# Reading a row of 120 indices as three separated rows of 40 in the one-hot comparisons of a graph network

## The chip, the cores and the metric

The kernel runs on one core of one Trainium2 chip. The metric is device microseconds of one execution. A profile of one execution shows what each engine did: PE is TensorE (PEld its weight loads), DVE is VectorE, ACT is ScalarE, POOL is GpSimd, SP is SyncE. An instruction is named by its line in the kernel, and operands by the program's tile names.

## What is computed

The reference is a relational graph network of three layers with 6250 nodes, 256 features, 100000 edges sorted by their target node `dst`, 32 attributes per edge and 3 edge types, followed by a residual and a layer norm:

```python
ew = edge_attr @ edge_w + edge_b
rel_masks = [(edge_type == i) for i in range(3)]
inv_cnt = [1.0 / maximum(segment_sum(m, dst), 1.0) for m in rel_masks]
for l in range(3):
    msg = relu(x[src] * ew)
    out = 0
    for i in range(3):
        h = segment_sum(msg * rel_masks[i][:, None], dst) * inv_cnt[i][:, None]
        out = out + h @ weights[l, i]
    out = out + x @ roots[l] + biases[l]
    x = x + relu(out)
result = layernorm(x_in + x)
```

## The kernel before, in words

Edges are worked on 128 at a time; two such blocks make a pair, and two pairs (four blocks, 512 edges) make the group that most instructions handle at once. There are 391 pairs, so 195.5 groups in a layer and 586.5 in the three layers. All state but the node rows stays in SBUF.

For one pair, `gather_pair` (its DMA is line L1053) issues two indirect DMAs from POOL's queue, each of which fetches the 128 rows `x[src]` of one block; `xs` is the tile they land in, with eight buffers of one group each (for the first six pairs of a layer the rows are fetched early). For one group:

- `seed_ew` (L621, ScalarE) and `make_ew` (L634, TensorE) form the edge weights `ew_p` in PSUM;
- `weigh` multiplies them into the rows (L656, VectorE) and applies relu (L657, ScalarE); the last group of a layer is weighed in smaller pieces by `weigh_last` (L662, L663);
- `one_hot` (L669, VectorE) makes for each of the four blocks a matrix `oh` of 128 edges by `WK` = 120 columns. Column r*40+w is one where the edge has type r and its target is w nodes above the base of its span. It is one `tensor_scalar` per block: the row `iota_w` of the numbers 0 to 119, the same in every partition, is compared for equality with one number per partition, a column of `seg`. In layer 0 ScalarE also makes a bf16 copy `oh_b` (L673), from which the edges are counted;
- `reduce` multiplies rows and one-hot matrices on TensorE (L687 or L695) and so sums the messages by node and type into a PSUM tile `h_p`;
- for each span of nodes `add` (L723, VectorE) adds `h_p` into `acc`, a ring of nodes in SBUF.

Once a block of 128 nodes has all its edges, `node_mul` (L754) applies the weights, `node_end` (L785, L788) scales, adds and writes the new rows to `x_mid` in DRAM (L791), from which the next layer's gathers read. The root product goes through `root_turn`, `root_mul` and `root_keep` (L739). The last layer normalises (L794 to L806) and writes out.

The order on each engine is the order in which the Python code issues the instructions (`tc.manual_schedule()`): a loop over steps of one pair calls the functions above with fixed offsets. At step `it` the pair at position it+9 is gathered, it+3 weighed, it+2 one-hot encoded and it reduced. In a step VectorE gets the weighing first, then what belongs to nodes, then the one-hots of a group, and last the adds.

`iota_w` is made once, ahead of everything else, by one GpSimd iota instruction (L1081).

Of the kernel before, what the change touches and what calls it, by code (L numbers as in the profile page):

```python
# [8 lines left out]
F32 = mybir.dt.float32  # L9
# [433 lines left out]
def ordered_path(ctx, tc, x, attr_laid, A, weights, roots, biases, edge_w, edge_b, out, src, src_i, seg, place_i, consts, x_root,  # L443
# [6 lines left out]
    nc = tc.nc  # L450
    P = 128
    N, D = x.shape
    E = src.shape[0]
    L, R = weights.shape[:2]
# [5 lines left out]
    DC = D // P  # L460
    WK = R * WIN
    AHEAD = 9
# [3 lines left out]
    for u, (lo, hi) in enumerate(zip(least, most)):  # L466
        if u < order[0]:
            reach.append((ASIDE + lo, ASIDE + hi))
        elif lo // RING == hi // RING:
            reach.append((lo % RING, hi % RING))  # L470
        else:
            reach.append((0, RING - 1))
    ident, ones, iota_w = consts
# [33 lines left out]

    acc = big.tile([P, DC + 1, R, ASIDE + 2 * P + WIN], F32, name="acc")
    inv = big.tile([P, NT, R], F32, name="inv")
# [6 lines left out]
    for c in range(DC + 1):  # L516
        if c < DC // 2:
            nc.vector.memset(acc[:, c], 0.0)
        else:
            nc.scalar.activation(acc[:, c].rearrange("p r n -> p (r n)"),  # L520
                                 zero.to_broadcast([P, R * (ASIDE + 2 * P + WIN)]), AF.Copy)
    nc.vector.memset(x_all[:, NT - 1, :], 0.0)
# [27 lines left out]
    def closes(u):  # L550
        p = order.index(u)
        return p == U - 1 or span_of[order[p + 1]] != span_of[u]
# [34 lines left out]
    def layer(l, r_sb, b_sb, ats, early, pools):  # L587
# [11 lines left out]
        xs, ew_ps, ohs, h_ps, h_ss, o_ps, rs = {}, {}, {}, {}, {}, {}, {}  # L599
# [13 lines left out]
        def pairs_of(q):  # L613
            return range(min(2, U - 2 * q))
# [50 lines left out]
        def one_hot(q):  # L665
            ohs[q] = edge.tile([P, 4, WK], F32, name="oh", bufs=3)
            n = 2 * len(pairs_of(q))
            for t in reversed(range(n)):
                nc.vector.tensor_scalar(ohs[q][:, t, :], iota_w, seg[:, 4 * q + t:4 * q + t + 1], None,  # L669
                                        op0=ALU.is_equal)  # L670
            if l == 0:
                oh_bs[q] = edge.tile([P, 4, WK], BF, name="oh_b", bufs=3)
                nc.scalar.activation(oh_bs[q][:, :n], ohs[q][:, :n], AF.Copy)  # L673

        def reduce(u):
# [8 lines left out]
            if turned(span):  # L684
                for i in range(2):
                    t = u % 2 * 2 + i
                    nc.tensor.matmul(h_p[:WK, :D], ohs[u // 2][:, t, :], xs[u // 2][:, u % 2, i, :],  # L687
                                     start=(i == 0 and first), stop=(i == 1 and closes(u)), skip_group_check=True)
                    if l == 0:
                        nc.tensor.matmul(h_p[:WK, D:D + 1], oh_bs[u // 2][:, t, :], full_ones[:, 0:1],  # L690
                                         start=False, stop=(i == 1 and closes(u)), skip_group_check=True)
                return
            for i in range(2):
                for d in range(CH):
                    nc.tensor.matmul(h_p[:, d * WK:(d + 1) * WK],  # L695
                                     xs[u // 2][:, u % 2, i, d * P:(d + 1) * P] if d < DC else full_ones,
# [15 lines left out]
        def add(span):  # L712
            u = span[0]
            if places[:1] != [u // 8]:
# [6 lines left out]
                                       skip_runtime_bounds_check_because="it is a place in acc")  # L721
            there = acc[:, :CH, :, bass.ds(place, WIN)]
            nc.vector.tensor_tensor(there, h_ps[span][:, :CH * WK].rearrange("p (c r w) -> p c r w", c=CH, r=R), there, op=ALU.add)  # L723
# [36 lines left out]
        def slot_of(c):  # L760
            return c % (RING // P) * P if c > 1 else ASIDE + c * P

# [4 lines left out]
        def wrap():  # L767
            nc.vector.tensor_add(acc[:, :CH, :, :WIN], acc[:, :CH, :, :WIN], acc[:, :CH, :, RING:ASIDE])

        def clear(slot):  # L770
            nc.scalar.activation(acc[:, :CH, :, slot:slot + P],  # L771
                                 zero[:, :, None, None].to_broadcast([P, CH, R, P]), AF.Copy)
            if slot == 0:
                nc.scalar.activation(acc[:, :CH, :, RING:ASIDE], zero[:, :, None, None].to_broadcast([P, CH, R, WIN]),
                                     AF.Copy)
# [52 lines left out]
        for it in range(-11, max(starts) + 8):  # L828
# [75 lines left out]
            if pair(2) is not None and first_of(it + 2, 2) and pair(2) // 2 != order[-1] // 2:  # L904
                one_hot(pair(2) // 2)
            if pair(3) is not None and first_of(it + 3, 2) and pair(3) // 2 == order[-1] // 2:
                one_hot(pair(3) // 2)
# [12 lines left out]


WIN = 40
RING = 1024
ASIDE = RING + WIN
ROOTS = 24
# [81 lines left out]
def schedule(N, E, share):  # L1007

    P = 128
    U = -(-E // (2 * P))  # L1010
    NT = -(-N // P)
    K = first_pairs(N, E)
    spans = spans_of(N, E)
    order = order_of(N, E)
    added = {s: p + 1 for s, p in stages(N, E, share)[2].items()}
    done = []
    for c in range(NT):
        edges = E * min(1.0, (P * (c + 1) / N) ** 0.5)
        u = U if c == NT - 1 else min(U, -(-int(edges) // (2 * P)) + 4)
        done.append(max(added[s] for s in spans if s[0] >= K and (s[0] < u or s[0] == K)))  # L1020
    node = lambda e: int(N * min(1.0, max(0.0, e / E)) ** 2)
    least = [node(2 * P * u - ASTRAY) for u in range(U)]
    most = [node(2 * P * u + ASTRAY) for u in range(U)]
    moved = done[1] + 1
    starts = [0] * NT
    step = moved
    for c in range(2, NT):
        step = starts[c] = max(done[c] + 2, step + 4)
    starts[1] = max([step + 4] + [added[s] for s in spans if s[0] < K and any(most[u] + WIN > P for u in range(*s))])
    starts[0] = max(max(added.values()), starts[1] + 4)  # L1030

    for u, v in spans:
        p = added[u, v]
        if u >= K:
            assert all(p <= starts[c] or least[u] >= P * (c + 1) for c in range(2, NT))
            assert p <= moved or least[u] >= 2 * P
            assert all(p < starts[c] or least[u] >= P * c for c in range(8, NT, 8))
            for b in range(RING // P + 1, (most[u] + WIN - 1) // P + 1):
                assert (moved + 2 if b - RING // P == 1 else starts[b - RING // P] + 4) < p
        else:  # L1040
            assert most[u] <= 2 * P and (p <= starts[1] or most[u] + WIN <= P)
    return order, starts, moved, least, most
# [16 lines left out]
def kernel(ctx, tc, x, src, dst, edge_attr, edge_type, weights, roots, biases, edge_w,  # L1059
# [3 lines left out]
    nc = tc.nc  # L1063
    P = 128
# [4 lines left out]
    T = (E + P - 1) // P  # L1069
    T -= T % -2  # L1070
    U = T // 2
    WK = 3 * WIN
    K = schedule(N, E, 1)[0][0]

    keep = ctx.enter_context(tc.tile_pool(name="keep", bufs=1))
# [1 line left out]
    make_identity(nc, ident)  # L1077
    ones = keep.tile([1, P], F32, name="ones_o")
    nc.vector.memset(ones, 1.0)
    iota_w = keep.tile([P, WK], F32, name="iota_w")  # L1080
    nc.gpsimd.iota(iota_w, pattern=[[1, WK]], base=0, channel_multiplier=0,  # L1081
                   allow_small_or_imprecise_dtypes=True)
    node_i = keep.tile([P, 1], F32, name="node_i")
    nc.gpsimd.iota(node_i, pattern=[[0, 1]], base=0, channel_multiplier=1, allow_small_or_imprecise_dtypes=True)
# [1 line left out]
    seg = keep.tile([P, TC], F32, name="seg_o")  # L1086
# [6 lines left out]
    with tc.tile_pool(name="look", bufs=1) as look, tc.tile_pool(name="look_p", bufs=2, space=PSUM) as look_p, \  # L1093
# [27 lines left out]
        base = look.tile([1, U], F32, name="base")  # L1121
# [103 lines left out]
```

## Time and profile before

| | |
|---|---|
| median of 3 runs | 2968.16 us (2967.99 to 2969.02) |
| the profiled execution's own time | 2969.27 us |
| its span, first to last instruction | 2967.0 us |
| mean granted TensorE clock | 0.971 |
| what DMA moved | 387.39 MB, mean 131 GB/s |
| costliest VectorE line | L656, 711.5 us in 585 instructions |
| costliest ScalarE line | L657, 615.7 us in 585 instructions |

The profile counts an engine as busy only while one of its instructions runs. A group of instructions is shown with its number, its busy time in us, the mean duration of one in ns, and the idle time of the engine just ahead of them with what ended it; "issue" there is time in which the engine waited for nothing that the profile shows. In a timeline the first number of a row is the start in us from the start of the span and the second the time in us; rows of the same kind that follow each other are merged (x4), and the idle time before stands in brackets. The time of an execution is a little longer than the span, since it has work ahead of the first and behind the last instruction.

### The profile page before, as it was taken

To read this page: it belongs to the slowest core of one execution; us is meant where nothing else is said; L and a number is where in the kernel's file an instruction comes from. 1 tells how busy PE (TensorE), PEld (TensorE's weight loads), DVE (VectorE), ACT (ScalarE), POOL (GpSimd) and SP (SyncE) were. 2 spreads that over 40 slices of the span, in tenths; PEclk is the share of its full clock that TensorE was granted. 3 is DMA by queue.
4 is the path that set the end of the run, shared out by engine and by line. 5 is a ranking of instruction groups with operands and counts; after the bars stand their busy time and mean duration, and the time that the engine had idled before them with its cause. 6 is when DMAs were issued, how large, how long until landed. Compare 5 with 4: busy or idle time off the path is not lost.

```text
span 2967.0 us, 43407 instructions
## 1 busy us (share of the span) xinstructions
PE 2588.4 (87%) x13712; PEld 1780.6 (60%) x13712; DVE 1886.0 (64%) x4910; ACT 1502.6 (51%) x1911; POOL 2235.0 (75%) x2355
## 2 busy tenths in 40 slices
PE   5999999999998788888988998778888988999886
PEld 2666677777765545555666666454555666666644
DVE  6656577777774545556666666445556677778754
ACT  4666656556565444454444444434444444444443
POOL 7777777777777777777777777777777777777776
PEclk9999999999999999999999999989999999999999
DMA  5444444444444444444444444444444444444443
GB/s 168 147 145 136 147 123 124 128 130 130 127 135 128 132 116 120 128 121 123 127 125 130 130 131 128 135 132 124 126 133 133 135 132 132 139 136 137 128 127 96
DMA packets 173705, 387.39 MB, mean 131 GB/s; under 512 B 43594, under 2 KB 79068, under 8 KB 173468
## 3 DMA queue, kind: packets, MB, share of 16 engines
q0 software_dynamic: 112608, 307.65, 36.1%
q1 hardware_dynamic: 53280, 68.50, 7.2%
q10 hardware_dynamic: 7580, 8.37, 0.9%
q8 instruction: 113, 1.85, 0.3%
q14 instruction: 124, 1.02, 0.1%
HBM read 364.89 MB, written 19.46 MB: 130 GB/s over the span
## 4 chain that ended last, share of the span: by engine, by line
PE 43%; DMA 17%; POOL 15%; issue 13%; DVE 7%; ACT 4%; DVEq 0%; POOLq 0%; ACTq 0%
POOL xs L1053 15%; DMA xs<-x_mid,src_r 14%; PE h_p L695 11%; PE ew_p L634 10%; PE h_p L687 9%; PE o_p L754 7%; DVE xs L656 5%; DMA xs<-in_x_dram,src_io 3%; PE r_p L736 3%; ACT xs L657 2%; ACT ew_p L621 2%; PE r_p L728 1%; PE h_p L707 1%; DVE x_root L739 1%; DVE acc L723 1%
## 5 line engine op out<-in xcount | busy, mean ns | idle before, releaser
L1053 POOL DMA_INDIRECT xs<-x_mid,src_r x1540 | 1465.5, 952 | 469.2 <-issue 367.8
L657 ACT ACTIVATE xs<-xs 128x1024 f32<-128x1024 f32 (+1 forms) x585 | 615.7, 1052 | 1315.7 <-DVE xs L656 1301.3
L656 DVE TENSOR_TENSOR xs<-ew_p,xs 128x1024 f32<-128x1024 f32 (+1 forms) x585 | 711.5, 1216 | 772.8 <-DMA xs<-x_mid,src_r 490.1
L1053 POOL DMA_INDIRECT xs<-in_x_dram,src_io x770 | 733.3, 952 | 235.1 <-issue 192.8
L695 PEld LDWEIGHTS h_p<-oh,xs 128*128 128x128 f32 x5160 | 663.5, 194 | 242.9 <-issue 114.5
L695 PE MATMUL h_p<-oh,xs 128*128 128x120 f32 x5160 | 725.7, 285 | 82.2 <-issue 36.6
L634 PE MATMUL ew_p<-ew_sb,at 64*128 64x512 f32 x2346 | 686.2, 661 | 101.0 <-ACT ew_p L621 96.9
L687 PE MATMUL h_p<-xs,oh 128*120 128x256 f32 x2088 | 575.4, 410 | 19.5 <-issue 5.7
L621 ACT ACTIVATE ew_p<-seed 128x1024 f32<-128x1024 f32 x582 | 588.8, 1012 | 0.0
L669 DVE TENSOR_SCALAR oh<-iota_w,seg_o 128x120 f32<-128x120 f32 x2346 | 512.6, 296 | 0.0
L754 PE MATMUL o_p<-w_sb,acc 128*128 128x256 f32 (+1 forms) x1728 | 440.1, 391 | 34.6 <-DVE x_root L785 31.2
L687 PEld LDWEIGHTS h_p<-xs,oh 128*120 128x120 f32 x2088 | 367.2, 193 | 161.9 <-issue 51.3
L723 DVE TENSOR_TENSOR acc<-h_p,acc 128x240 f32 (+1 forms) x732 | 323.7, 442 | 191.0 <-PE o_p L754 70.5
L754 PEld LDWEIGHTS o_p<-w_sb,acc 128*128 128x128 f32 (+1 forms) x1728 | 308.1, 190 | 158.6 <-DVE x_root L785 71.4
L634 PEld LDWEIGHTS ew_p<-ew_sb,at 64*128 64x128 f32 x2346 | 181.3, 189 | 230.6 <-ACT ew_p L621 124.5
L785 DVE SCALAR_TENSOR_TENSOR x_root<-o_p,inv,x_root 128x256 f32<-128x256 f32 (+1 forms) x432 | 207.0, 479 | 27.9 <-PE o_p L754 21.0
L736 PE MATMUL r_p<-r_sb,t_s 128*128 128x256 f32 x588 | 161.6, 398 | 33.0 <-ACT t_s L732 32.2
L771 ACT ACTIVATE acc<-zero_o 128x768 f32<-128x768 f32 (+1 forms) x150 | 140.2, 934 | 14.6 <-PE o_p L754 13.9
L673 ACT ACTIVATE oh_b<-oh 128x480 bf16<-128x480 f32 x196 | 116.2, 593 | 45.3 <-DVE oh L669 43.6
L736 PEld LDWEIGHTS r_p<-r_sb,t_s 128*128 128x128 f32 x588 | 103.5, 193 | 54.8 <-ACT t_s L732 43.1
L728 PEld LDWEIGHTS r_p<-ident_o,x_all 128*128 128x128 f32 x294 | 30.7, 143 | 167.3 <-DVE x_root L739 121.0
L728 PE MATMUL r_p<-ident_o,x_all 128*128 128x128 f32 x294 | 65.0, 303 | 69.2 <-DVE x_root L739 68.9
(110 smaller groups left out, 942.8 us busy)
## 6 DMA issues: line engine op xcount, KB each, us to landing
at<-in_attr_laid_dram SPq DMA_DIRECT2D x147, 256.0 KB
xs<-x_mid,src_r POOLq DMA_INDIRECT x1540, 2.8
xs<-in_x_dram,src_io POOLq DMA_INDIRECT x770, 2.8
x_mid<-x_all SPq DMA_DIRECT2D x96, 128.0 KB
x_all<-in_x_dram ACTq DMA_DIRECT2D x8, 768.0 KB
x<-in_x_dram SPq DMA_DIRECT2D x48, 128.0 KB
out_dram<-x_all SPq DMA_DIRECT2D x48, 128.0 KB
w_sb<-in_L_gnn_weights_dram SPq DMA_DIRECT2D x3, 768.0 KB
```

Source lines behind the costliest of these rows:

```text
L621: nc.scalar.activation(ew_ps[q][:, :n], seed[:, None, :, :].to_broadcast([P, n, 2, D]), AF.Copy)
L634: nc.tensor.matmul(ew_ps[q][:, k].rearrange("p i d -> p (i d)"), at[half, :], ew_sb[half].rearrange("p i d -> p (i d)"), start=False, stop ...
L656: nc.vector.tensor_mul(there, ew_ps[q][:, pairs.start:pairs.stop], there)
L657: nc.scalar.activation(there, there, AF.Relu)
L669: nc.vector.tensor_scalar(ohs[q][:, t, :], iota_w, seg[:, 4 * q + t:4 * q + t + 1], None, op0=ALU.is_equal)
L687: nc.tensor.matmul(h_p[:WK, :D], ohs[u // 2][:, t, :], xs[u // 2][:, u % 2, i, :], start=(i == 0 and first), stop=(i == 1 and closes(u)), ...
L695: nc.tensor.matmul(h_p[:, d * WK:(d + 1) * WK], xs[u // 2][:, u % 2, i, d * P:(d + 1) * P] if d < DC else full_ones, (ohs if d < DC else o ...
L723: nc.vector.tensor_tensor(there, h_ps[span][:, :CH * WK].rearrange("p (c r w) -> p c r w", c=CH, r=R), there, op=ALU.add)
L736: nc.tensor.matmul(rs[c][:, 1, :], t_ss[c][:, d, :], r_sb[:, d, :], start=(d == 0), stop=(d == DC - 1))
L754: nc.tensor.matmul(o_p[:n, j, :], acc[:, d, r, slot:slot + n], w_sb[:, r * DC + d, :], start=(d == 0), stop=(d == DC - 1))
L785: nc.vector.scalar_tensor_tensor(root, o_p[:n, j, :], inv[:n, c, r:r + 1], root, op0=ALU.mult, op1=ALU.add)
L1053: nc.gpsimd.indirect_dma_start(out=xs[:, u % 2, i, :], out_offset=None, in_=x_rows[:, :], in_offset=bass.IndirectOffsetOnAxis(ap=src_i[:, ...
```

## The change

The tile `iota_w` gets three rows of 44 numbers in place of one row of 120. In each row the first 40 places hold the numbers (0 to 39, 40 to 79, 80 to 119), and the last 4 are never read or written. The comparison reads the three rows of 40, and its output is written as before, 120 numbers next to each other, now addressed as three rows of 40 that touch. The same numbers are compared with the same numbers.

```diff
@@ one_hot
             for t in reversed(range(n)):
-                nc.vector.tensor_scalar(ohs[q][:, t, :], iota_w, seg[:, 4 * q + t:4 * q + t + 1], None,
+                nc.vector.tensor_scalar(ohs[q][:, t, :].rearrange("p (r w) -> p r w", r=R), iota_w[:, :, :WIN], seg[:, 4 * q + t:4 * q + t + 1], None,
                                         op0=ALU.is_equal)
@@
 WIN = 40
+APART = WIN + 4
@@ tile_gnn_resnorm_kernel
-    WK = 3 * WIN
@@
-    iota_w = keep.tile([P, WK], F32, name="iota_w")
-    nc.gpsimd.iota(iota_w, pattern=[[1, WK]], base=0, channel_multiplier=0,
+    iota_w = keep.tile([P, 3, APART], F32, name="iota_w")
+    nc.gpsimd.iota(iota_w[:, :, :WIN], pattern=[[WIN, 3], [1, WIN]], base=0, channel_multiplier=0,
                    allow_small_or_imprecise_dtypes=True)
```

## The prediction

> **What bounds the kernel now.** I read the page's top and its chain of waits first.
>
> ```profile
> span 2967.0 us, 43407 instructions
> PE 2588.4 (87%) x13712; PEld 1780.6 (60%) x13712; DVE 1886.0 (64%) x4910; ACT 1502.6 (51%) x1911; POOL 2235.0 (75%) x2355
> PE 43%; DMA 17%; POOL 15%; issue 13%; DVE 7%; ACT 4%; DVEq 0%; POOLq 0%; ACTq 0%
> ```
>
> By busy share and by the chain, TensorE looks like the bound. The groups of line L1053, the gathers that POOL issues, say otherwise (busy us, mean ns, then idle us ahead; in the second view min/median/max ns, first and last start):
>
> ```profile
> L1053 POOL DMA_INDIRECT xs<-x_mid,src_r x1540 | 1465.5, 952 | 469.2 <-issue 367.8 <-ACT ew_p L621 35.7 <-PE r_p L728 11.0
> L1053 POOL DMA_INDIRECT xs<-in_x_dram,src_io x770 | 733.3, 952 | 235.1 <-issue 192.8 <-ACT ew_p L621 12.5 <-DMA xs<-in_x_dram,src_io 6.1
> L1053 POOL DMA_INDIRECT xs<-x_mid,src_r x1540: 942/947/1477, 1002.5 to 2951.0; - x193
> L1053 POOL DMA_INDIRECT xs<-in_x_dram,src_io x770: 942/946/1958, 19.1 to 986.3; - x193
> L1053 POOL DMA_INDIRECT x_root<-in_x_dram,src_f x12: 942/946/1111, 3.8 to 17.8; - x12
> L1053 POOLq EVENT_SEMAPHORE  x589: 17/43/6376, 16.8 to 2940.1; - x197
> ```
>
> The idle time is 469.2/1540 = 0.305 us for each gather of one group and 235.1/770 = 0.305 in the other: a fixed pause after each gather, not a wait. From the first start (3.8) to the last (2951.0), 2346 gathers follow each other at 2947.2/2345 = 1.257 us, against 0.947 + 0.305 = 1.252 for the median one. So POOL hands out gathers without a break from start to end, and all else follows: the "75%" is 952 of 1257 ns. The span is 3.8 us, the gathers, and 16.0 us of tail after the last one starts. Only what changes a gather's length, starves POOL, or lengthens the tail can move the time.
>
> What lengthens a gather? Its median is 947, its mean 952: 1465.5 - 1540 x 0.947 = 7.1 us and 733.3 - 770 x 0.946 = 4.9 us, together **12.0 us** above the median pace. I looked for these gathers in the timeline, and for Vector instructions that are stretched too:
>
> ```profile
> L669 DVE TENSOR_SCALAR oh<-iota_w,seg_o x2346: 249/275/520, 40.5 to 2952.6; 128x120 f32<-128x120 f32 x196
> L806 DVE TENSOR_SCALAR x_all<-x_all,mv x49: 411/413/648, 2118.6 to 2961.0; 128x256 f32<-128x256 f32 x48, 106x256 f32<-106x256 f32 x1
> L739 DVE TENSOR_TENSOR x_root<-r_p,b_sb x147: 404/414/416, 65.7 to 2737.6; 128x256 f32<-128x256 f32 x147
> L785 DVE SCALAR_TENSOR_TENSOR x_root<-o_p,inv,x_root x432: 466/482/486, 138.3 to 2958.8; 128x256 f32<-128x256 f32 x141, 106x256 f32<-106x256 f32 x3
> L788 DVE SCALAR_TENSOR_TENSOR x_all<-x_root,x_all x147: 424/425/499, 145.6 to 2959.3; 128x256 f32<-128x256 f32 x144, 106x256 f32<-106x256 f32 x3
> ```
>
> The two TENSOR_SCALAR lines, one SBUF input and an SBUF output, have a long upper tail (520 and 648 over medians of 275 and 413). L739 and L785, with one tensor in PSUM, have none (416 and 486). L788, with two in SBUF, has a short one. L669 is the one-hot comparison, and it is the line that the change rewrites. Both sides of the blocking are visible:
>
> ```profile
> 1438.30 1.07 DVE L669 TENSOR_SCALAR oh<-iota_w,seg_o 128x120 f32<-128x120 f32 x4
> 1438.38 0.95 POOL L1053 DMA_INDIRECT xs<-x_mid,src_r  x1 [0.30 <-PE ew_p L634]
> 1851.72 0.85 DVE L669 TENSOR_SCALAR oh<-iota_w,seg_o 128x120 f32<-128x120 f32 x4
> 1852.06 1.32 POOL L1053 DMA_INDIRECT xs<-x_mid,src_r  x1 [0.30 <-issue]
> ```
>
> In the first pair four one-hots take 1.07 us in place of 0.85 and the gather is untouched. In the second the one-hots keep 0.85 and the gather takes 1.32 in place of 0.95. Over the whole timeline, 231 gathers are over 8 ns longer than the median; 199 of them overlap a one-hot and carry 12.7 us of the 13.9 us of excess; in 169 of these (8.2 us) no other Vector instruction with two SBUF inputs or of the L806 kind overlaps, in 30 (4.6 us) one does.
>
> [...]
>
> **The change part by part.** (a) The index row gets gaps. POOL's one iota still makes 120 numbers:
>
> ```profile
> L1081 POOL IOTA iota_w<- 128x120 f32 x1 | 0.2, 226 | 0.0
> L1053 POOL DMA_INDIRECT x_root<-in_x_dram,src_f x12 | 11.6, 969 | 4.8 <-issue 3.4 <-DMA src_f<-in_src_laid_dram 1.5
> ```
>
> It stands ahead of the first gather, which waits 1.5 us for its indices: cost nothing; without that cover at most its own 0.2 us.
>
> (b) All 2346 one-hots read three rows of 40 that do not touch, and write 120 numbers that do. No trace row shows such a pair. [...]
>
> ```profile
> L577 DVE TENSOR_SCALAR src_r<-src_io 128x782 int32<-128x782 int32 x1 | 0.6, 558 | 0.0
> L578 DVE SCALAR_TENSOR_TENSOR src_r<-src_io,src_r 128x782 int32<-128x782 int32 x1 | 1.0, 974 | 0.0
> L669 DVE TENSOR_SCALAR oh<-iota_w,seg_o 128x120 f32<-128x120 f32 x2346 | 512.6, 296 | 0.0
> ```
>
> (974 - 558)/782 = 0.53 ns an element, x 120 = 64 ns: a one-hot goes from 275 to about 339 ns, four from 0.85 to 0.85 + 4 x 0.064 = 1.11 us. Today's mean for four is 512.6/586.5 = 0.874 with the blocking in it, so VectorE works 0.235 us more per four, 586.5 x 0.235 = 138 us, and reaches about 2024 us or 68%. The lower bound for (b) is nothing (rate unchanged). VectorE is not the bound, so in a steady stretch this hides under the 5.02 us that four gathers take.
>
> (c) Gathers are no longer blocked by one-hots. Bounds: nothing, and all 12.0 us. I take the 8.2 us, and half of the 4.6 (the two-input instructions stay): **-10.5 us**.
>
> (d) Where the longer one-hots show. POOL starves once, for a row tile at the start:
>
> ```profile
> 57.89 0.95 POOL L1053 DMA_INDIRECT xs<-in_x_dram,src_io  x1 [0.30 <-issue]
> 59.62 0.95 POOL L1053 DMA_INDIRECT xs<-in_x_dram,src_io  x1 [0.79 <-ACT t_s L732]
> ```
>
> That is 0.79 - 0.30 = 0.49 us, behind a chain with some four groups of one-hots since 40.5 us: 0 to 4 x 0.26 = 1.0 us more, taken **+0.5**. At the end of a layer the last rows of x_mid leave well before they are gathered:
>
> ```profile
> 996.44 0.33 SPq L791 DMA_DIRECT2D x_mid<-x_all  x1
> 1002.54 0.99 POOL L1053 DMA_INDIRECT xs<-x_mid,src_r  x1 [0.30 <-issue]
> DMA to landing us min/median/max: 2.6/2.8/6.8
> ```
>
> 6.1 us, less a landing (nearest row: the gathers' median of 2.8), cover one group's 0.26. In the tail the group stands between two weighings:
>
> ```profile
> 2951.01 0.95 POOL L1053 DMA_INDIRECT xs<-x_mid,src_r  x1 [0.30 <-issue]
> 2952.06 0.85 DVE L669 TENSOR_SCALAR oh<-iota_w,seg_o 128x120 f32<-128x120 f32 x4
> 2952.82 0.42 DVE L662 TENSOR_TENSOR xs<-ew_p,xs 128x256 f32<-128x256 f32 x1
> 2953.74 0.42 DVE L662 TENSOR_TENSOR xs<-ew_p,xs 128x256 f32<-128x256 f32 x1 [0.51 <-DMA xs<-x_mid,src_r]
> ```
>
> The second L662 waits 0.51 us for the last gather's landing, more than 0.26: nothing.
>
> Sum: -10.5 + 0.5 = -10.0 us. The profiled execution took 2969.27, 2.3 outside its span, and should become 2959.3; the median of the runs, 2968.16, is 1.1 lower, so **2958.2**.
>
> **Rivals.** [...]
>
> *B, layer 0 falls behind (slower).* TensorE is nearly full there, and the add into acc (L723), on which it waits, is queued on VectorE right behind the one-hots:
>
> ```profile
> 300.00:650.00 350.00, 333.91 (x2061) 243.93 (x2060) 246.04 (x624) 210.01 (x271) 264.99 (x280) 1.00 0.45 131
> 650.00:870.00 220.00, 211.73 (x1315) 155.67 (x1315) 164.30 (x418) 131.93 (x160) 166.68 (x176) 1.00 0.44 130
> PEld h_p L695 <- DVE acc L723: 22.4, 24, 1.9
> 817.33 0.22 PE L695 MATMUL h_p<-oh_b,full_ones 128*128 128x120 bf16 x1
> 826.84 0.96 POOL L1053 DMA_INDIRECT xs<-in_x_dram,src_io  x1 [0.30 <-ACT ew_p L621]
> ```
>
> PE is 95% and 96% busy; the third row is of 556 to 865 us. The last two are the tightest place after the start: the gather at 826.84 refills the tile that the matmul at 817.33 was last to read (found by counting the matmuls of L687 and L695), a margin of 9.3 us. From 300 to 870 us 113 groups pass; with the full 0.235 us on the path they lose 26.6 us, POOL stalls for 26.6 - 9.3 = 17.3, and the time is 2958.2 + 17.3 = 2975. Stalling begins above 0.08 us per group, a net loss above (9.3 + 10.0)/113 = 0.17. Against it: these are 24 waits in the 309/5.02 = 61 groups of their stretch; if the 0.235 reaches the path in those alone, it is 0.09 us per group, about where stalling begins and far from a loss.
>
> *C, part of the blocking stays*, because any Vector traffic from SBUF disturbs POOL: a third of the gain, 2965. L739 and L785 without a tail speak against it.
>
> **How the numbers follow.** Forecast 0.69, its own range 2955.5 (all 12.0 us and the 0.49) to 2963 (half the gain); A 0.13, B 0.10, C 0.08. The range 2955.5 to 2968.5 takes in the forecast, C and half of A. A change of 0.2% is 5.9 us, about what a measurement can tell: under 2962.2 lies nearly all of the forecast, 0.68; between that and 2974.1 lie A, C and a little of B, 0.22; above, 0.10.
>
> **What would show it.** Right: L669 at about 339 ns with hardly any spread between median and maximum; L1053's mean near 947 to 948 with the pause still 0.305; VectorE near 68%; the last gather starting near 2941. [...] Wrong by B: idle time ahead of L1053 above 0.305 a gather, between 600 and 900 us. Wrong by C: L669 at a narrow 339 and L1053's mean still 950 or more.

## The result, and the profile after

The changed kernel takes 2960.94 us in the median (2959.04 to 2962.46, 10 runs) against 2968.89 (2967.99 to 2970.57, 10 runs): a ratio of **0.9973, 95% interval 0.9965 to 0.998**, or 8.0 us less. The forecast was 10.0 us less. The profiled execution after, 2962.46 us, is the slowest of its ten runs and 6.8 us below the profiled one before, 2969.27. The rows below come from these two executions.

The profiled execution has a span of 2960.2 us in place of 2967.0. Its engines (the head of the page), and the gathers, whose line is now L1054: first their groups with busy us, mean ns and idle us, then min/median/max ns with first and last start.

```profile
span 2960.2 us, 43407 instructions
PE 2591.9 (88%) x13712; PEld 1782.6 (60%) x13712; DVE 1998.2 (68%) x4910; ACT 1503.8 (51%) x1911; POOL 2228.8 (75%) x2355
```

```profile
L1054 POOL DMA_INDIRECT xs<-x_mid,src_r x1540 | 1460.5, 948 | 469.1 <-issue 363.4 <-ACT ew_p L621 31.1 <-PE h_p L687 11.3
L1054 POOL DMA_INDIRECT xs<-in_x_dram,src_io x770 | 732.0, 951 | 234.6 <-issue 192.3 <-ACT ew_p L621 11.0 <-DMA xs<-in_x_dram,src_io 5.8
```

```profile
L1054 POOL DMA_INDIRECT xs<-x_mid,src_r x1540: 942/946/1455, 1000.9 to 2944.3; - x193
L1054 POOL DMA_INDIRECT xs<-in_x_dram,src_io x770: 942/946/2007, 19.1 to 984.5; - x193
```

Two things stand in these rows. VectorE works 1998.2 - 1886.0 = 112 us *more*, and the kernel is faster. And POOL's gathers are busy 1465.5 - 1460.5 = 5.0 and 733.3 - 732.0 = 1.3 us less, 6.3 together, with the pause after each still 469.1/1540 = 0.305 us. The last gather starts at 2944.3 in place of 2951.0, which is 6.7 of the span's 6.8 us: 6.3 are the shorter gathers, and the rest is the one starvation of POOL, 0.49 us at 59.62, which did not come back. The timeline of POOL after shows only the usual pause there.

```profile
58.45 0.94 POOL L1054 DMA_INDIRECT xs<-in_x_dram,src_io  x1 [0.30 <-issue]
59.69 0.95 POOL L1054 DMA_INDIRECT xs<-in_x_dram,src_io  x1 [0.30 <-issue]
60.95 0.95 POOL L1054 DMA_INDIRECT xs<-in_x_dram,src_io  x1 [0.30 <-issue]
```

The run with two rows apart, below, whose comparisons last as long as before, does not have that starvation either (0.30 us ahead of its gather at 59.45). So its absence is not shown to be the change's doing.

The durations of the rewritten comparison and of the three Vector lines beside it, in the form of the prediction's rows:

```profile
L669 DVE TENSOR_SCALAR oh<-iota_w,seg_o x2346: 303/327/335, 40.8 to 2946.2; 128x120 f32<-128x120 f32 x196
L806 DVE TENSOR_SCALAR x_all<-x_all,mv x49: 411/414/647, 2113.6 to 2954.3; 128x256 f32<-128x256 f32 x48, 106x256 f32<-106x256 f32 x1
L739 DVE TENSOR_TENSOR x_root<-r_p,b_sb x147: 406/414/417, 64.1 to 2731.6; 128x256 f32<-128x256 f32 x147
L788 DVE SCALAR_TENSOR_TENSOR x_all<-x_root,x_all x147: 424/425/483, 144.0 to 2952.6; 128x256 f32<-128x256 f32 x144, 106x256 f32<-106x256 f32 x3
```

L669 went from 249/275/520 to 303/327/335: longer in the median, and its tail is gone. L806, which was not touched, keeps its tail of 647.

**What a held gather looks like.** From the timeline after, two gathers that are still held, each with the Vector instruction that runs as it starts (start us, duration us):

```profile
98.41 1.35 DVE L765 TENSOR_TENSOR acc<-acc 128x1152 f32<-128x1152 f32 x1
98.57 2.01 POOL L1054 DMA_INDIRECT xs<-in_x_dram,src_io  x1 [0.30 <-PE h_p L690]
871.62 0.43 DVE L788 SCALAR_TENSOR_TENSOR x_all<-x_root,x_all 128x256 f32<-128x256 f32 x1
871.67 1.19 POOL L1054 DMA_INDIRECT xs<-in_x_dram,src_io  x1 [0.30 <-issue]
```

L788 ends at 872.05, 0.38 us into the gather, and the gather is 1.19 - 0.95 = 0.24 us too long. L765 ends at 99.76, 1.19 us into its gather, which is 1.06 us too long. Both fit one reading of these profiles: the gather's wait ends with the Vector instruction that is in progress some **0.13 us after the gather's start**. Being in progress there is not enough, however. In the profiles before, after and of the changed kernel once more (below), 166 gathers have an L788 alone in progress at that point. The 48 whose L788 had started 45 ns or more ahead of them are all longer, each by the L788's end less 0.13 us to within 12 ns. The 118 whose L788 had started later, from 42 ns ahead on, are at most 3 ns longer. (The limit is L788's own: after, two L768's that started 26 and 28 ns ahead did hold their gathers.) The seven L788's of the profiles before and after that are in progress at that point and started 2 to 42 ns ahead of the gather are themselves the longer ones (458 to 499 ns over a median of 425), here 0.48 in place of 0.43 us:

```profile
1898.15 0.48 DVE L788 SCALAR_TENSOR_TENSOR x_all<-x_root,x_all 128x256 f32<-128x256 f32 x1
1898.18 0.95 POOL L1054 DMA_INDIRECT xs<-x_mid,src_r  x1 [0.30 <-issue]
```

I sorted all gathers more than 8 ns over 947 by the Vector line in progress at that point. Before: 8.0 us of excess lie under L669 (164 gathers, alone or overlapping its neighbour), 1.7 under L788, 1.5 under L765, 0.4 under L768, 0.3 under L806. After: less than 0.1 under L669 alone, 2.7 under L788, 1.7 under L765, 0.9 under L768, 0.7 under L806. Of the gathers with an L669 alone in progress there, 131 of 338 were held before and 6 of 423 after, these by at most 12 ns.

### The profile page after: what moved, and what is told of

It is laid out like the page before. It is cut to its first block, busy times and chain, and to the rows that moved or that the text cites. A ratio compares the mean times of both kernels' runs of the same rounds, so it can differ in the third digit from the quotient of the medians.

```text
span 2960.2 us, 43407 instructions
## 1 busy us (share of the span) xinstructions
PE 2591.9 (88%) x13712; PEld 1782.6 (60%) x13712; DVE 1998.2 (68%) x4910; ACT 1503.8 (51%) x1911; POOL 2228.8 (75%) x2355
## 5 line engine op out<-in xcount | busy, mean ns | idle before, releaser
L1054 POOL DMA_INDIRECT xs<-x_mid,src_r x1540 | 1460.5, 948 | 469.1 <-issue 363.4
L1054 POOL DMA_INDIRECT xs<-in_x_dram,src_io x770 | 732.0, 951 | 234.6 <-issue 192.3
L695 PE MATMUL h_p<-oh,xs 128*128 128x120 f32 x5160 | 734.3, 287 | 86.4 <-issue 34.5
L669 DVE TENSOR_SCALAR oh<-iota_w,seg_o 128x120 f32<-128x120 f32 x2346 | 622.9, 327 | 0.0
```

The costliest lines, as they stand in the source:

```text
L669: nc.vector.tensor_scalar(ohs[q][:, t, :].rearrange("p (r w) -> p r w", r=R), iota_w[:, :, :WIN], seg[:, 4 * q + t:4 * q + t + 1], None, o ...
L695: nc.tensor.matmul(h_p[:, d * WK:(d + 1) * WK], xs[u // 2][:, u % 2, i, d * P:(d + 1) * P] if d < DC else full_ones, (ohs if d < DC else o ...
L1054: nc.gpsimd.indirect_dma_start(out=xs[:, u % 2, i, :], out_offset=None, in_=x_rows[:, :], in_offset=bass.IndirectOffsetOnAxis(ap=src_i[:, ...
```

## The experiments

All runs are compared with the kernel before on the same chip at the same time. A gather's ordinary length is not the same in all profiles: its median is 946 or 947 ns in the two above, in the second one of the changed kernel and in that of the kernel before with more comparisons, and 949 ns in the other five, of which one (two rows apart) has comparisons as long as before. Summed over the ordinary gathers (those not more than 8 ns over 947) that is some 4 to 6 us; so ratios are compared, not microseconds across sessions. The row of the run with the sum in PSUM, below:

```profile
L1055 POOL DMA_INDIRECT xs<-x_mid,src_r x1540: 942/949/1456, 1000.3 to 2945.6; - x193
```

**The changed kernel again**

> The changed kernel once more, as the mark for the others. Every theory: about 2961 us, ratio 0.997 to before; comparisons (L669) near 327 ns without a tail; gathers' mean near 949 ns.

Ratio 0.9973 (0.9963 to 0.9984), median 2967.02 us against 2974.61. L669 again without a tail:

```profile
L669 DVE TENSOR_SCALAR oh<-iota_w,seg_o x2346: 304/328/335, 39.5 to 2944.0; 128x120 f32<-128x120 f32 x196
L1054 POOL DMA_INDIRECT xs<-x_mid,src_r x1540 | 1459.5, 948 | 469.1 <-issue 362.2 <-ACT ew_p L621 32.6 <-DMA xs<-x_mid,src_r 11.0
```

The excess over 947 ns, summed over all gathers (those below it counted as negative), is 3.5 us here, 5.4 in the first profile of the same kernel, and 11.5 before. What is left depends on where in a gather the few remaining instructions fall.

**Two rows apart in place of three**

```diff
-  ohs[q][:, t, :].rearrange("p (r w) -> p r w", r=R), iota_w[:, :, :WIN]
+  ohs[q][:, t, :].rearrange("p (r w) -> p r w", r=2), iota_w[:, :, :60]
-  iota_w = keep.tile([P, 3, APART], F32, name="iota_w")
+  iota_w = keep.tile([P, 2, 64], F32, name="iota_w")
```

(The iota that fills the tile is changed to match.)

> The index row in two rows of 60 with a gap of 4 between them, in place of three of 40. [...] Rival (the gap itself helps, by keeping the row out of the way of POOL or by shortening each run): L669 stays near 327 ns without a tail and the time near 2961 us.

Ratio 0.9998 (0.9989 to 1.0007): the gain is gone. The rows of L669 and of the gathers:

```profile
L669 DVE TENSOR_SCALAR oh<-iota_w,seg_o x2346: 249/275/514, 40.8 to 2957.4; 128x120 f32<-128x120 f32 x196
L1054 POOL DMA_INDIRECT xs<-x_mid,src_r x1540 | 1468.7, 954 | 469.5 <-issue 357.6 <-ACT ew_p L621 37.8 <-DMA xs<-x_mid,src_r 11.0
```

The durations are those of before to the nanosecond in the median, with the tail. So this gap in the index row does nothing by itself (275 ns). Three rows of 40 apart against an output of 120 in a row took 327 ns; the next run has two more pairs of shapes. The gathers' mean of 954 includes the longer ordinary gather (949) of that profile.

**Which shapes last longer**

```diff
+  nc.vector.tensor_scalar(spare[:, 0, :, :WIN], iota_w[:, :, :WIN], seg[:, 4 * q:4 * q + 1], None, op0=ALU.is_equal)
+  nc.vector.tensor_scalar(spare[:, 1, :, :WIN], iota_c.rearrange("p (r w) -> p r w", r=R), seg[:, 4 * q + 1:4 * q + 2], None, op0=ALU.is_equal)
```

(`spare` has rows of 40 apart, `iota_c` is the old row of 120; both comparisons are added to the changed kernel and nobody reads them.)

> The changed kernel with two spare comparisons per group that differ in shape: one reads three rows of 40 apart and writes three rows of 40 apart, the other reads 120 in a row and writes three rows of 40 apart. [...] If what counts is the input alone: the first 327, the second 275 with a tail.

The two spare comparisons (L672 three rows apart on both sides, L674 a gap in the output alone):

```profile
L672 DVE TENSOR_SCALAR spare<-iota_w,seg_o x588: 280/293/512, 42.7 to 2956.3; 128x120 f32<-128x120 f32 x196
L674 DVE TENSOR_SCALAR spare<-iota_c,seg_o x588: 310/322/328, 42.9 to 2956.5; 128x120 f32<-128x120 f32 x196
```

Three rows against three stay short: 293 ns, 18 over the 275 of one row against one, with a tail to 512; 31 gathers (1.9 us of excess) are held with L672 alone in progress at their 0.13 us point. One row against three lasts longer: 322 ns, no tail (328 at most). So it is not the input alone. Of all the pairs measured, one row against one lasts 275 ns, two rows of 60 apart against one 275 and three of 40 apart against three apart 293, each with a tail; three apart against one last 327 and one against three apart 322, without. Why these are shorter or longer is not shown. The run was timed once, so its time (2972.2 us) has no interval.

**More VectorE work of the new form**

```diff
+  spare = edge.tile([P, 2, WK], F32, name="spare", bufs=1)
+  for t in range(2):
+      nc.vector.tensor_scalar(spare[:, t, :].rearrange("p (r w) -> p r w", r=R), iota_w[:, :, :WIN], seg[:, 4 * q + t:4 * q + t + 1], None, op0=ALU.is_equal)
```

> The changed kernel with two more comparisons per group, of the same form, into a scratch tile that nobody reads, ahead of the adds into acc: 2 x 0.245 x 586.5 = 287 us more of VectorE, 77% busy. [...] Rival (the longer VectorE work is on the path everywhere, the change would have won more with shorter comparisons): a tenth of 287 us or more, ratio above 1.01.

Ratio 0.9971 (0.996 to 0.9983), the same as without them (0.9973) and below the rival's 1.01. The engines, the spare comparisons, and the gathers:

```profile
PE 2592.4 (87%) x13712; PEld 1782.5 (60%) x13712; DVE 2273.9 (77%) x6086; ACT 1503.8 (51%) x1911; POOL 2234.0 (75%) x2355
L673 DVE TENSOR_SCALAR spare<-iota_w,seg_o x1176: 319/328/339, 41.4 to 2952.4; 128x120 f32<-128x120 f32 x196
L1058 POOL DMA_INDIRECT xs<-x_mid,src_r x1540 | 1464.8, 951 | 469.5 <-issue 380.2 <-ACT ew_p L621 23.2 <-PE h_p L691 9.8
L1058 POOL DMA_INDIRECT xs<-in_x_dram,src_io x770 | 732.8, 952 | 234.8 <-issue 194.5 <-ACT ew_p L621 9.1 <-PE h_p L699 4.9
```

VectorE has 276 us more than the changed kernel and the time does not move. The pause after each gather stays 0.305 us in both rows, so POOL was not starved, not even in layer 0. The means of 951 and 952 contain the longer ordinary gather, 949 here: the excess over each profile's own median is 5.9 us, against 7.7 and 5.8 in the two profiles of the changed kernel.

**More VectorE work of the old form**

```diff
+      nc.vector.tensor_scalar(spare[:, t, :], iota_w, seg[:, 4 * q + t:4 * q + t + 1], None, op0=ALU.is_equal)
```

(two more comparisons a group, in the same place, added to the kernel before in its own form, one row of 120 against one)

> [...] Rival (the excess comes from POOL's own course, not from the comparisons): gathers' mean stays 952 ns, ratio 1.000.

Ratio 1.0042 (1.0025 to 1.0059), some 12 us slower, where the rival had 1.000.

```profile
PE 2587.2 (87%) x13712; PEld 1779.5 (60%) x13712; DVE 2107.7 (71%) x6086; ACT 1502.9 (50%) x1911; POOL 2249.0 (75%) x2355
L673 DVE TENSOR_SCALAR spare<-iota_w,seg_o x1176: 261/275/441, 40.8 to 2966.2; 128x120 f32<-128x120 f32 x196
L1057 POOL DMA_INDIRECT xs<-x_mid,src_r x1540 | 1475.2, 958 | 469.2 <-issue 367.7 <-ACT ew_p L621 32.3 <-ACT xs L657 11.0
```

Summed over all gathers the excess is 25.5 us against 11.5 before. In proportion to the number of comparisons, half as many again, the 8.0 us under L669 before would have grown by some 4 us (an estimate); the whole grew by 14.0. It does not follow the number: 232 of the 264 gathers with a spare comparison in progress at their 0.13 us point are held, but before, with twice as many of the others, 168 of 388 (whatever else overlaps). So the price depends on where the comparisons fall against a gather. This pair of runs carries the verdict: six comparisons of the old form take less VectorE time than six of the new form (2107.7 against 2273.9 us in all) and cost 0.7% more.

**What still holds the gathers**

```diff
+  ends = part == len(parts_of(c)) - 1 and j == len(parts_of(c)[part]) - 1
-  nc.vector.scalar_tensor_tensor(root, o_p[:n, j, :], ...)
+  nc.vector.scalar_tensor_tensor(o_p[:n, j, :] if ends else root, o_p[:n, j, :], ...)
-  nc.vector.scalar_tensor_tensor(x_all[:n, c, :], root, 0.0, x_all[:n, c, :], op0=ALU.max, op1=ALU.add)
+  nc.vector.scalar_tensor_tensor(x_all[:n, c, :], o_p[:n, j, :], 0.0, x_all[:n, c, :], op0=ALU.max, op1=ALU.add)
```

> The changed kernel, and the last weighted sum of each node block is written into PSUM, so that L788 (now some lines on) has one input in PSUM and one in SBUF in place of two in SBUF. Theory (what blocking is left comes from Vector instructions with two SBUF inputs that run while a gather wants to read, some 130 ns after its start; in the changed kernel 2.7 us of the 5.4 us of excess lie under L788): its 2.7 us go, 2958 us, gathers' mean about 948 ns. Rival (the excess that is left has nothing to do with the inputs' place): 2961 us, as the changed kernel.

Ratio 0.9967 (0.9955 to 0.9979); the medians of the same session are 2964.69 against 2967.02 for the changed kernel. The old L788, now L789:

```profile
L789 DVE SCALAR_TENSOR_TENSOR x_all<-o_p,x_all x144: 423/425/426, 144.6 to 2954.1; 128x256 f32<-128x256 f32 x141, 106x256 f32<-106x256 f32 x3
```

With one of its inputs in PSUM it lasts as long as ever (425) but its maximum falls from 483 to 426. In 57 of its 147 places it covers a gather's 0.13 us point, and in 17 of these it had started 45 ns or more ahead; the 57 gathers have 0.02 us of excess together, none over 7 ns. In the changed kernel there were 57 such places too, 19 of them with that start, and 2.7 us. The trace shows the effect of the input's place; the 2.3 us between the medians alone would not, since the intervals overlap.

**In pieces**

```diff
-  there = acc[:, :CH, :, ASIDE + P:ASIDE + 2 * P]
-  nc.vector.tensor_add(there, there, acc[:, :CH, :, P:2 * P])
+  for d in range(CH):
+      there = acc[:, d, :, ASIDE + P:ASIDE + 2 * P]
+      nc.vector.tensor_add(there, there, acc[:, d, :, P:2 * P])
```

(on top of the sum in PSUM; the addition of L768 is cut in the same way)

> As the run with the sum in PSUM, and the additions of acc to acc (L765 and L768, 1.7 and 0.9 us of excess in the changed kernel) are cut into two or three pieces, one for each 128 columns of features. Theory (a gather is held until the Vector instruction in progress ends): if it gets in between two pieces, 1 to 1.7 us less than the run with the sum in PSUM, 2956.5 to 2957.5 us; if pieces that follow each other directly hold it as one, no gain, 2958 us. Rival (the excess is not the instructions'): 2961 us.

Ratio 0.9962 (0.9948 to 0.9975), median 2963.41 us (2962.93 to 2964.55): the lowest of that session, below the changed kernel's 2967.02 and the 2974.61 before. The pieces of the two additions:

```profile
L766 DVE TENSOR_TENSOR acc<-acc x7: 545/550/569, 98.5 to 2054.0; 128x384 f32<-128x384 f32 x7
L770 DVE TENSOR_TENSOR acc<-acc x42: 252/274/289, 298.3 to 2820.1; 128x120 f32<-128x120 f32 x42
```

Their excess is 0.5 and 0.4 us, against 0.8 and 0.6 in the run with the sum in PSUM. That difference is within what differs between two profiles of one kernel. But gathers do get in between pieces, as two places show:

```profile
98.46 1.50 DVE L766 TENSOR_TENSOR acc<-acc 128x384 f32<-128x384 f32 x3
98.91 0.95 POOL L1057 DMA_INDIRECT xs<-in_x_dram,src_io  x1 [0.31 <-issue]
2053.57 1.02 DVE L766 TENSOR_TENSOR acc<-acc 128x384 f32<-128x384 f32 x2
2053.87 1.08 POOL L1057 DMA_INDIRECT xs<-x_mid,src_r  x1 [0.31 <-PE r_p L728]
```

The first gather takes its ordinary 0.95 us amid three pieces that end at 99.96. The second is 0.13 us too long: the first piece ends 0.26 us into it, the second one 0.72. At 1073.75, 2416.38 and 2540.80 us a gather waited for the next piece as well. So cutting helps in some places, and what it is worth in time is not shown. Against the changed kernel the ranges of the single runs overlap (its runs go from 2960.59 to 2969.17), so the order of those two rests on the medians and on the excess under L788.

## Why the prediction was right

The time, 2960.94, lies in the forecast's own range (2955.5 to 2963), and the cause is the one named. Point by point:

- *POOL sets the pace.* Held: the last gather starts 6.7 us earlier, which is nearly all of the span's 6.8, and 276 us more VectorE work cost nothing.
- *(a) The index row costs nothing.* Held: the first gather still starts at 3.8 us.
- *(b) A comparison goes from 275 to 339 ns.* The direction was right, the size 12 ns too high: 327, a step of 52 ns in place of 64. So VectorE gained 112 us in place of 138, and stands at 68% as forecast. The 64 ns were an estimate from the difference of L578 and L577; no run shows that what separates those two lines also separates the two forms of the comparison, and what the runs showed is the 52. That the input is no single run is not enough for it: two rows of 60 apart are none either, and keep 275 ns.
- *(c) 10.5 of the 12.0 us of excess go.* **This is the mis-sized term**: 6.3 went in that profile by the same sum over rows. That the longer form would not hold the gathers was taken, not shown, beforehand; the runs showed it: what lay under the comparisons went whole, 8.0 us, to less than 0.1. But I took half of the "mixed" 4.6 us for the comparisons' own and expected the rest to stand still; the excess under the instructions with two SBUF inputs and L806 grew instead, from 3.9 to 6.0 us under L788, L765, L768 and L806 (the figures above). The number of L788's that cover the sensitive point hardly moved (51 before, 55 after, alone at that point), nor did the number that held a gather (15 and 17). Where within the gather these end changed: on average 115 ns past the point before and 157 after. The second profile of the changed kernel has 1.9 us less excess than the first, 8.0 less than before. The term was sized from one profile as if those few instructions always fell alike.
- *(d) The start costs 0.5 more.* Wrong in sign: the starvation of 0.49 us was absent after. By the run with two rows apart that is chance, not a gain of the change, and it makes up for part of what (c) took too high. The end of a layer and the tail cost nothing, as forecast: the span's end lies 15.9 us after the last gather's start, against 16.0.
- *Rival A* (the comparisons stay nearly as short and go on holding the gathers) did not come about: L669 went to 327 ns without a tail. No run shows the term that its time was worked out from; what the runs showed in its place is that three rows apart on both sides last 293 ns, 18 over the 275, with a tail to 512, and do hold gathers (31 of them, 1.9 us).
- *Rival B* (layer 0 falls behind): the margin of 9.3 us at its tightest became 8.5, counted in the same way. With the spare comparisons VectorE had (2273.9 - 1886.0)/586.5 = 0.66 us more per group than before, and POOL still was not starved, its margin there being some 5.5 us (the gather at 826.07, after the matmul that starts at 820.30). So the longer work reaches TensorE's path there only in small part; my worst case had all of it there.
- *Rival C* (any Vector traffic holds POOL): refuted by the spare comparisons of the new form, 1176 of them without a tail (339 at most), and by L789 (426 at most, 0.02 us of excess).

## What to carry to other kernels

When one queue hands out work without a break, price a change by what it does to one step of that queue, not by engine shares: here VectorE became 6% busier and the kernel faster. Look for spread: here a comparison of fixed size whose maximum (520 ns) was far above its median (275) was being held by something, and its partner, the gather, held in turn (1.32 in place of 0.95 us), was on the bound. More comparisons of three rows against one cost nothing here (VectorE at 77%, ratio 0.9971 against 0.9973), and more of those of one row against one cost 0.4% of the time (1.0042), though each is shorter (275 against 328 ns). The L788's, with two inputs in SBUF, had 2.7 us of the gathers' excess under them, and 0.02 us with one input in PSUM.

## What I had not expected of the hardware

- What holds a gather does so at one point of it, not over its whole length. A gather of 947 ns is held at a point some 130 ns after its start, if the Vector instruction was there first, and waits for it to end (1.06 us behind an L765); behind one-hots that follow each other it can wait for more than one (the gather at 1852.06 of the prediction has the third of the four in progress at that point and waits until the fourth ends, 0.5 us into it). A comparison of one row against one is held in turn mostly late in a gather: in the kernel before, 32 of the 33 that started 500 to 525 ns into one had a median of 480 ns, and none of them ended later than 1000 ns into it. It is also held a little at the start: 29 of the 83 that started 46 to 87 ns ahead of a gather took 301 to 342 ns, and these all ended 253 to 256 ns into it. No comparison was held for a whole gather: the longest of the 2346 took 520 ns.
- The place of an input counts at the same shape and duration: with both inputs in SBUF (L788, 425 ns) the gathers under it had 2.7 us of excess, with one of them in PSUM (L789, 425 ns) 0.02 us.
- The ordinary length of a gather is 946 ns in some profiles and 949 in others, with either form of comparison, which is some 4 to 6 us of this kernel's time and nearly as much as the change itself. Why is open.
